# A two-layer Mamba-and-experts kernel: layer 0's first sequence ahead of the rest, other rows and the router between scan units, idle TensorE products at the start, an expert per six units

## The chip, the cores and the metric

The kernel runs on one core of one Trainium2 chip, in fp32 apart from small counts in bf16. The metric is the device time of one execution in microseconds, the median over runs. A core has five engines that run side by side, each with an instruction queue of its own worked in order: TensorE (PE: matrix products, whose weight loads are listed as PEld), VectorE (DVE), ScalarE (ACT), GpSimd (POOL) and SyncE (SP), which here only issues transfers. They wait for each other through semaphores.

## The reference, cut to what matters

The input x is 8 sequences of 256 tokens with 128 features, 2048 rows in all. Two layers follow each other. In both, the normalized x goes through an attention-like part and a mixture of experts, and both are added to x. Layer 0 has a selective state-space model (256 channels, 16 states each) and 8 experts that each choose 512 tokens; layer 1 has a retention block and 16 experts, of which each token chooses two. The change is in layer 0:

```
xn = _layernorm(x)                     # outer norm
x = x + _L0_attn_ref(xn, ...) + _L0_ffn_ref(xn, ...)

# _L0_attn_ref, X = xn
Xn = (X - mu) * rsqrt(var + 1e-05) * ln_g + ln_b         # inner norm
X_main = einsum('bld,ed->ble', Xn, W_up1)
X_main = silu(causal_conv4(X_main, conv_w) + conv_b)
pp = einsum('bld,ed->ble', X_main, W_ll) + b_ll
delta = softplus(pp[..., :D]); Bm = pp[..., D:D+N]; Cm = pp[..., D+N:]
A = -exp(A_log)
A_bar = exp(delta * A)
U = X_main * (A_bar - 1) / (delta * A) * delta * Bm
for t in range(256):                   # the scan
    H = A_bar[t] * H + U[t]
    y[t] = sum_n(C[t] * H)
Y = y * silu(einsum('bld,ed->ble', Xn, W_up2))
out = X + einsum('bld,ed->ble', Y, W_down) + b_down

# _L0_ffn_ref, xt = rows of xn
scores = softmax(xt @ Wr)              # 2048 x 8, the router
G, idx = top_k(scores.T, 512)          # each expert takes 512 rows
h = gelu(xt[idx] @ W1 + b1); X_e = h @ W2 + b2
out = zeros.at[idx].add(G * X_e)
```

## The kernel before

`block_kernel` writes both layers into one program. Layer 0 is written under a manual schedule: on PE, ACT, DVE and POOL the instructions stand in the order in which the Python code emits them. Only SP's transfers are ordered by the tile framework. Line numbers below are those of the kernel before.

**Ahead of the scan.** SP loads x in four parts (L187) and then the parameters, one after the other. DVE takes mean and variance of the 16 row blocks of 128 rows (L233, L234). ACT and DVE make `rs` and, for the second norm inside the state-space part, `nm` and `rv`. For each quarter of the rows (512 rows, two sequences) ACT writes the inner norm `xh` and DVE the outer norm `xn`; PE transposes both; `XnT` (for the state-space part) and `xnT` (for the router) are the copies out of PSUM. `xn` goes to DRAM (`xn_d`), from which experts later gather rows. POOL prepares `wcv`, the four convolution taps times the up projection, and `dg`, diagonal matrices with 1/A. Then come the router's products (`pl`, L736), its softmax, and the search.

**The search** (`search`, L427) finds each expert's 512th score in ten steps of three bits: DVE makes seven candidates, compares all scores (`ge`) and adds them up (`cp`), PE adds over partitions (`pc`), and DVE keeps what still has 512 rows (`keep`, `m`, `thr`). Then it ranks the chosen rows. It is a Python generator: each `next` emits the part up to the next `yield`. In the same way `front(q)` (L303) emits the front of block q (two sequences) in ten parts: convolution products `pu`, gate products `pg`, silu, `pd` for delta, `pbc` for B and C, the softplus, `BT` with B transposed, and `xT` and `xS`, the transposed inputs. ACT needs one function table for silu, another for exp and ln, and another for gelu; each change of table is an instruction of its own.

**Units.** The loop `for k in range(len(units) + 4)` at the end of layer 0 runs over 64 units: 8 sequences, 4 groups of 4 states, 2 halves of the channels. A unit is a pipeline over several passes of the loop: `spread_b` (POOL, `Bd`), `decays` two passes ahead (ACT, `ab`), `x_times_b` one pass ahead (PE, `u`), `steps` (DVE: `u` times `ab - 1`, then the scan into `h`), `times_c` one pass later (POOL), `sums` two passes later (PE, `py`). After eight units `gated` and `down` finish a sequence. C comes back from DRAM spread over all partitions (`Cb`, three buffers).

Beside the unit each pass emits one part of each generator in `running`: the search, `base` (POOL adds xn and a bias to x, which is then written to `acc_d`), a front (block 1 from pass 0, 2 from 17, 3 from 33), and `select(e)`, which every `PACE` = 5 passes starts to find and gather expert e's rows. As soon as the first expert's rows are there, each pass also emits a part of `experts()`: five parts per expert, the first with both halves of the hidden layer, then four output products; results are scattered with addition into `acc_d` by POOL. Six of the ten search steps are emitted ahead of the loop, between parts of `front(0)`.

**Shared storage.** `bank()` gives PSUM tiles out of two buffers, shared by fronts, router, search, select and experts; `u` has two PSUM buffers of its own, `ab` three and `h` four in SBUF. `x` and `xn` share their SBUF place with the hidden tiles `ht` of the experts, `xh` and `xnT` with the experts' gathered rows `XgT`.

Layer 1 follows (from L839): it reads `acc_d` back, when all scatters have landed.

Of the kernel before, what the change touches and what calls it, by code (L numbers as in the profile page):

```python
# [8 lines left out]
F32 = mybir.dt.float32  # L9
# [16 lines left out]
K = 4  # L26
# [16 lines left out]
SB = 3  # L43
BK = 64
# [6 lines left out]
def block_kernel(ctx: ExitStack, tc: tile.TileContext, a: dict, out: bass.AP):  # L51
# [98 lines left out]
    with ExitStack() as l0:  # L150
# [13 lines left out]

        def exp_and_ln():

            nc.scalar.add_instruction(
                mybir.InstLoadActFuncSet(
                    name=nc.get_next_instruction_name(), act_func_set_id=EXP_LN, ins=[], outs=[]
                )  # L170
            )
# [16 lines left out]
        alog = load0("alog", [P, ND, N], a["alog"].rearrange("(c p) n -> p c n", p=P))  # L188
# [6 lines left out]
        ln_g = load0("ln_g", [P, 1])  # L195
        ln_b = load0("ln_b", [P, 1])
        wr0 = load0("wr0", [P, E0])
        conv_b = load0("conv_b", [P, ND])
# [6 lines left out]
        wup2 = load0("wup2", [P, D])  # L205
        wll = load0("wll", [P, ND, D + 2 * N], a["wll"].rearrange("(c p) e -> p c e", p=P))
        bll_d = load0("bll_d", [P, ND])
        bll_bc = load0("bll_bc", [2 * N, 1])
# [16 lines left out]
        exp_and_ln()  # L225
        nc.scalar.activation(An, alog, AF.Exp)
        nc.scalar.activation(sd[:, 0:1], eps_t, AF.Sqrt)
        nc.gpsimd.memset(XnT[:, :, 0 : K - 1], 0.0)
        for c in range(NC):
            if c == 8:  # L230
                nc.vector.tensor_scalar(An, An, -1.0, None, ALU.mult)
                nc.vector.reciprocal(rA, An)
            nc.vector.bn_stats(st[:, c, :], x[:, c, :])  # L233
            nc.vector.bn_aggr(mv[:, c, :], st[:, c, :])  # L234
        nc.scalar.activation(sd, mv[:, :, 1], AF.Sqrt, bias=eps_t)

        for dc in range(ND):
            for n in range(0, N, 8):
                nc.gpsimd.tensor_tensor(
                    dg[:, dc, n : n + 8], bc(eye, 1, 8), bc(rA[:, dc, n : n + 8], 2, BK), ALU.mult  # L240
                )
        nc.gpsimd.tensor_tensor(wcv, bc(wup1, 1, K), conv_w, ALU.mult)
        rs = main.tile([P, NC], F32, name="rs")
        nc.vector.reciprocal(rs, sd)
        vi = main.tile([P, NC], F32, name="vi")
        nc.vector.tensor_mul(vi, mv[:, :, 1], rs)
        nc.vector.tensor_mul(vi, vi, rs)
        nc.scalar.activation(vi, vi, AF.Sqrt, bias=eps_t)
        nm = main.tile([P, NC], F32, name="nm")
# [24 lines left out]
        for h in range(2):  # L274
            for g in range(2):
                q = 2 * h + g
                cols = slice(q * BLK, (q + 1) * BLK)
                for c in range(4 * q, 4 * q + 4):
# [4 lines left out]
                    if c:  # L283
                        normalize(c)
# [1141 lines left out]
```

## Time and profile before

The median of three runs is 700.51 us (699.24 to 701.1).

| what | us |
|---|---|
| profiled execution, its own time | 702.32 |
| its span, first to last instruction | 700.4 |
| first scan unit starts | 68.0 |
| unit 8 (search done) starts | 123.5 |
| unit 17 starts | 165.0 |
| last scan (unit 63) starts | 431.4 |
| layer 1 reads x back (`x<-acc_d`) | 442.6 |

Busy time in us in four stretches:

| stretch | length | PE | DVE | ACT | POOL |
|---|---|---|---|---|---|
| 0 to 41.5 | 41.5 | 22.3 | 23.1 | 16.3 | 8.8 |
| 41.5 to 68.0 | 26.5 | 21.0 | 19.1 | 16.4 | 8.0 |
| 68.0 to 123.5 | 55.5 | 42.2 | 51.7 | 26.4 | 32.4 |
| 345.9 to 395.8 | 49.9 | 46.5 | 35.9 | 30.1 | 44.7 |

A line of the list of groups names the source line, engine, operation and tiles (out <- in), how many there are, then busy time and the mean in ns, then the idle time just ahead of them and who ended most of it. A line of the timeline begins with start and duration in us; in brackets stands how long the engine was idle and who released it. In the page's rows of digits each digit is the busy share of one fortieth of the span in tenths.

### The profile page before, as it was taken

Reading aid. Unit: us, or ns where it says so; the run is one execution under the profiler, and the core shown is the slowest. Engines: PE = TensorE matmul, PEld = TensorE weight load, DVE = VectorE, ACT = ScalarE, POOL = GpSimd, SP = SyncE. Lnnn points to the kernel's source line nnn. Section 1 sums busy time; section 2 is a strip of 40 time slices with the busy share of each in tenths; the row PEclk is TensorE's granted clock in tenths of the full one; section 3 lists DMA queues with packets and bytes.
Section 4 is the critical chain, followed back from the end, with each engine's and each line's share of the span. In section 5 each row is a group of like instructions: output and inputs, shape, how many; then the busy total and the mean of one; then the engine's idle time right before and its main releaser. Section 6 shows DMA issues by size and latency. Waiting matters only on the chain.

```text
span 700.4 us, 14519 instructions
## 1 busy us (share of the span) xinstructions
PE 560.8 (80%) x5721; PEld 427.5 (61%) x5721; DVE 428.2 (61%) x669; ACT 332.5 (47%) x763; POOL 381.8 (55%) x320
## 2 busy tenths in 40 slices
PE   0997777789889798989798867497639899999980
PEld 0765545667666776756675756364215498999870
DVE  7367998997647578465666887565117532454333
ACT  2546355556677574677374731243003243555530
POOL 5004646698868789873999896106740022444340
PEclk9997887789989899998898987567558888999995
DMA  7813002222692343321332220122424246888306
GB/s 206 106 24 122 32 31 103 82 78 71 143 181 67 95 108 80 85 60 50 84 96 76 60 80 2 60 91 87 153 84 152 71 128 210 286 276 288 139 27 183
DMA packets 59859, 76.27 MB, mean 109 GB/s; under 512 B 14992, under 2 KB 43808, under 8 KB 59536
## 3 DMA queue, kind: packets, MB, share of 16 engines
q1 hardware_dynamic: 51632, 65.81, 32.6%
q0 software_dynamic: 8160, 9.54, 6.4%
q8 instruction: 45, 0.74, 0.4%
q14 instruction: 22, 0.18, 0.1%
HBM read 59.46 MB, written 13.78 MB: 105 GB/s over the span
## 4 chain that ended last, share of the span: by engine, by line
PE 34%; DVE 10%; issue 9%; POOL 7%; ACT 3%; DMA 2%; SPq 0%; POOLq 0%; DVEq 0%; ACTq 0%
PE ph L1175 6%; PE py L1189 5%; PE py L705 3%; POOL h L696 3%; PE ps L1008 3%; PE u L670 2%; PE pret L1028 2%; DVE u L688 2%; PE ph L603 2%; PE po L621 2%; DVE h L692 2%; POOL acc_d L569 2%; DMA y<-y_d 1%; POOL xg L546 1%; DVE st L1015 1%
## 5 line engine op out<-in xcount | busy, mean ns | idle before, releaser
L696 POOL TENSOR_TENSOR h<-h,Cb 128x1024 f32<-128x1024 f32 x64 | 172.2, 2727 | 32.3 <-DVE h L692 17.4
L692 DVE TENSOR_TENSOR_SCAN h<-ab,u 128x1024 f32<-128x1024 f32 x64 | 146.4, 2287 | 6.3 <-DVE ab L690 0.5
L680 ACT ACTIVATE ab<-delta,An 128x256 f32<-128x256 f32 x256 | 108.5, 498 | 23.2 <-DVE h L692 22.3
L1195 POOL DMA_INDIRECT y_d<-yo,xt x47 | 45.4, 967 | 119.1 <-DVE yo L1194 107.9
L688 DVE SCALAR_TENSOR_TENSOR u<-ab,u 128x1024 f32<-128x1024 f32 x64 | 78.0, 1218 | 48.1 <-PE u L670 33.1
L705 PE MATMUL py<-h,dg 64*64 64x128 f32 x2048 | 81.6, 302 | 23.0 <-POOL h L696 17.3
L670 PE MATMUL u<-Bd,xT 64*128 64x128 f32 x512 | 84.7, 311 | 12.2 <-DVE h L692 11.5
L670 PEld LDWEIGHTS u<-Bd,xT 64*128 64x128 f32 x512 | 71.1, 212 | 29.0 <-issue 14.1
L705 PEld LDWEIGHTS py<-h,dg 64*64 64x64 f32 x2048 | 64.0, 148 | 33.2 <-POOL h L696 21.1
L670 PE MATMUL u<-Bd,xS 64*128 64x128 f32 x512 | 82.3, 312 | 1.2 <-DMA xS<-xT 1.2
L1180 ACT ACTIVATE hid<-ph,wb 128x128 f32<-128x128 f32 x188 | 53.6, 368 | 51.9 <-issue 21.4
L670 PEld LDWEIGHTS u<-Bd,xS 64*128 64x128 f32 x512 | 68.7, 211 | 1.7 <-DMA xS<-xT 1.5
L569 POOL DMA_INDIRECT acc_d<-oc,idx x32 | 51.6, 1611 | 25.5 <-ACT oc L626 19.7
L1015 DVE TENSOR_TENSOR st<-ps,decay_sb 128x384 f32<-128x384 f32 x64 | 31.2, 548 | 52.6 <-remote 29.4
L1175 PE MATMUL ph<-xT,wb 128*128 128x128 f32 x376 | 53.6, 288 | 3.3 <-DVE xT L1169 2.7
L1124 POOL DMA_INDIRECT xs_d<-xk,pos x32 | 32.1, 1002 | 41.9 <-DVE hit L1106 32.5
L1175 PEld LDWEIGHTS ph<-xT,wb 128*128 128x128 f32 x376 | 48.8, 202 | 5.9 <-DVE xT L1169 3.1
L1189 PE MATMUL py<-wb,hid 128*128 128x128 f32 x376 | 51.2, 281 | 0.0
L654 POOL TENSOR_TENSOR Bd<-eye,BT 128x256 f32<-128x256 f32 x64 | 50.5, 992 | 0.0
L1189 PEld LDWEIGHTS py<-wb,hid 128*128 128x128 f32 x376 | 47.3, 198 | 0.0
L621 PEld LDWEIGHTS po<-w,ht 128*128 128x128 f32 x256 | 35.9, 209 | 14.9 <-issue 5.2
L621 PE MATMUL po<-w,ht 128*128 128x128 f32 x256 | 40.5, 303 | 4.5 <-ACT BT L388 2.8
(257 smaller groups left out, 900.9 us busy)
## 6 DMA issues: line engine op xcount, KB each, us to landing
wb<-in_bank_dram SPq DMA_DIRECT2D x47, 514.0 KB
Cb<-C_d SPq DMA_DIRECT2D x32, 512.0 KB
w<-in_w_dram SPq DMA_DIRECT2D x16, 256.0 KB
xs_d<-zrow SPq DMA_DIRECT2D x1, 3031.5 KB
xt<-xs_d SPq DMA_DIRECT2D x11, 260.0 KB
xS<-xT SPq DMA_DIRECT2D x16, 128.0 KB
y<-y_d SPq DMA_DIRECT2D x8, 256.0 KB
decay_sb<-in_decay_dram SPq DMA_DIRECT2D x1, 1536.0 KB
```

Source lines behind the costliest of these rows:

```text
L569: i = nc.gpsimd.indirect_dma_start(out=acc_d, out_offset=bass.IndirectOffsetOnAxis(ap=idx[:, e, s : s + 1], axis=0), in_=oc, in_offset=Non ...
L621: nc.tensor.matmul(po, ht[:, hc, s * P : (s + 1) * P], w2[:, hc, :], start=(hc == 0), stop=(hc == NH - 1),)
L654: nc.gpsimd.tensor_tensor(t[:, w], eye.unsqueeze(1).unsqueeze(1).to_broadcast([P, 2, 2, BK]), bc(BT[b // 2][:, j + 2 * i : j + 2 * i + 2, ...
L670: nc.tensor.matmul(U[k][:, 2 * r : 2 * r + 2, t0 : t0 + BK], xT[b][r ^ half][rows, c, dc * P : (dc + 1) * P], Bd[b, g][rows, 2 * c + half] ...
L680: nc.scalar.activation(ab[k][:, n, :], delta[b // 2][:, dc, (b % 2) * L : (b % 2 + 1) * L], AF.Exp, scale=An[:, dc, g * NG + n : g * NG + ...
L688: nc.vector.scalar_tensor_tensor(U[k], ab[k], -1.0, U[k], ALU.add, ALU.mult)
L692: return nc.vector.tensor_tensor_scan(hf, af, uf, 0.0, ALU.mult, ALU.add)
L696: nc.gpsimd.tensor_mul(hh[k][:, w], hh[k][:, w], Cb[b, g][:, w])
L705: nc.tensor.matmul(pyv[cols, i, dc, :], dg[rows, dc, g * NG + n, :], hh[k][rows, n, j * P : (j + 1) * P], start=(g == 0 and dc == 0 and n ...
L1175: nc.tensor.matmul(ph[:, hc, :], w[:, hc * P : (hc + 1) * P], xTs[t], start=True, stop=True)
L1180: nc.scalar.activation(hids[t][:, hc, :], ph[:, hc, :], AF.Relu, bias=w[:, DI + NH * DM + hc : DI + NH * DM + hc + 1],)
L1189: nc.tensor.matmul(py, hids[t][:, hc, :], w[:, DI + hc * DM : DI + (hc + 1) * DM], start=(hc == 0), stop=(hc == NH - 1),)
```

## The change

It does five things.

1. The start is cut. The first four row blocks get their variances and deviations ahead of the other twelve, only their `xh` and `XnT` are made, and `front(0, (0,))` emits the front of sequence 0 alone; its two `xS` copies are made by DVE out of PSUM instead of two transfers, and its gates come after the decays of units 0 and 1. Products on `ident` (`WARM` = 24) stand at the head of PE's queue. `wcv` and the parameter loads are ordered for this, `An`, `rA` and `dg` come after the first `pd`.
2. The front of sequence 1, `front(0, (1,))`, runs in the loop from pass 0; block 1's starts at pass 4 instead of 0.
3. A generator `others()` emits the other rows' norms and transposes, the router and all ten search steps inside the loop. The copies of `xnT` move from DVE to ACT.
4. While the search runs, each generator in `running` emits two parts per pass instead of one. `base` starts only after it.
5. `PACE` is 6; experts emit five parts in six passes, and the sixth has none.

By this, selecting begins at pass 10 (before: 8) and the first expert at pass 18 (before: 15).

```diff
--- before.py
+++ after.py
...
 ROW1 = DM + 2
...
-        alog = load0("alog", [P, ND, N], a["alog"].rearrange("(c p) n -> p c n", p=P))
+        ln_g = load0("ln_g", [P, 1])
+        ln_b = load0("ln_b", [P, 1])
         wup1 = load0("wup1", [P, D])
...
-        ln_g = load0("ln_g", [P, 1])
-        ln_b = load0("ln_b", [P, 1])
+        conv_b = load0("conv_b", [P, ND])
+        alog = load0("alog", [P, ND, N], a["alog"].rearrange("(c p) n -> p c n", p=P))
+        wll = load0("wll", [P, ND, D + 2 * N], a["wll"].rearrange("(c p) e -> p c e", p=P))
+        bll_d = load0("bll_d", [P, ND])
+        bll_bc = load0("bll_bc", [2 * N, 1])
+        wup2 = load0("wup2", [P, D])
         wr0 = load0("wr0", [P, E0])
-        conv_b = load0("conv_b", [P, ND])
...
-        wup2 = load0("wup2", [P, D])
-        wll = load0("wll", [P, ND, D + 2 * N], a["wll"].rearrange("(c p) e -> p c e", p=P))
-        bll_d = load0("bll_d", [P, ND])
-        bll_bc = load0("bll_bc", [2 * N, 1])
...
-        exp_and_ln()
-        nc.scalar.activation(An, alog, AF.Exp)
...
         nc.scalar.activation(sd[:, 0:1], eps_t, AF.Sqrt)
         nc.gpsimd.memset(XnT[:, :, 0 : K - 1], 0.0)
-        for c in range(NC):
-            if c == 8:
-                nc.vector.tensor_scalar(An, An, -1.0, None, ALU.mult)
-                nc.vector.reciprocal(rA, An)
+        nc.gpsimd.tensor_tensor(wcv, bc(wup1, 1, K), conv_w, ALU.mult)
...
+        def variance(c):
             nc.vector.bn_stats(st[:, c, :], x[:, c, :])
             nc.vector.bn_aggr(mv[:, c, :], st[:, c, :])
-        nc.scalar.activation(sd, mv[:, :, 1], AF.Sqrt, bias=eps_t)
-
-        for dc in range(ND):
...
-        nc.gpsimd.tensor_tensor(wcv, bc(wup1, 1, K), conv_w, ALU.mult)
...
-                transposes(h, 4 * g, xn, "xn")
-                nc.scalar.activation(
-                    XnT[:, 2 * q : 2 * q + 2, K - 1 :],
...
-                nc.vector.tensor_copy(
-                    xnT[:, cols], pts[h, "xn"][:, 4 * g : 4 * g + 4, :].rearrange("p j l -> p (j l)")
...
+        def deviations(cs):
+            nc.scalar.activation(sd[:, cs], mv[:, cs, 1], AF.Sqrt, bias=eps_t)
+            nc.vector.reciprocal(rs[:, cs], sd[:, cs])
+            nc.vector.tensor_mul(vi[:, cs], mv[:, cs, 1], rs[:, cs])
+            nc.vector.tensor_mul(vi[:, cs], vi[:, cs], rs[:, cs])
+            nc.scalar.activation(vi[:, cs], vi[:, cs], AF.Sqrt, bias=eps_t)
...
+        def inner(c):
+            nc.scalar.activation(
+                xh[:, c, :], x[:, c, :], AF.Identity, bias=nm[:, c : c + 1], scale=rv[:, c : c + 1]
+            )
...
+        def inner_rows(c0, n, name):
...
+            pt = bank(f"pt_xh{name}", [P, n, P])
+            for j in range(n):
+                nc.tensor.transpose(pt[:, j, :], xh[:, c0 + j, :], ident)
+            nc.scalar.activation(
+                XnT[:, c0 // 2 : (c0 + n) // 2, K - 1 :],
+                pt.rearrange("p (b j) l -> p b (j l)", j=2),
+                AF.Identity, bias=ln_b, scale=ln_g,
+            )
...
+        def outer(q):
+            for c in range(4 * q, 4 * q + 4):
+                nc.vector.tensor_scalar(
+                    xn[:, c, :], x[:, c, :], mv[:, c, 0:1], rs[:, c : c + 1], ALU.subtract, ALU.mult
+                )
...
+        def outer_rows(q):
+            pt = bank(f"pt_xn{q}", [P, 4, P])
+            for j in range(4):
+                nc.tensor.transpose(pt[:, j, :], xn[:, 4 * q + j, :], ident)
+            nc.scalar.copy(xnT[:, q * BLK : (q + 1) * BLK], pt.rearrange("p j l -> p (j l)"))
...
+        warm = bank("warm", [P, P])
+        for _ in range(WARM):
+            nc.tensor.matmul(warm, ident, ident, start=True, stop=True)
+        for c in range(4):
+            variance(c)
+        deviations(slice(0, 4))
+        for c in range(4, NC):
+            variance(c)
+        for c in range(2):
+            inner(c)
+        inner_rows(0, 2, "0a")
+        for c in range(2, 4):
+            inner(c)
+        deviations(slice(4, NC))
+        inner_rows(2, 2, "0b")
+
         xn_dv = xn_d.rearrange("(p c) d -> p c d", p=P)
-        nc.sync.dma_start(xn_dv[:, :, 0:DM], xn)
...
-        def front(q):
...
+        def front(q, hs=(0, 1)):
+
+            h0, n = hs[0], len(hs)
...
+            at_once = q == 0 and h0 == 0
+            if h0 == 0:
...
-                for h in range(2):
+                for h in hs:
...
-                        xq[:, dc, h * L : (h + 1) * L], pu, AF.Silu if q == 0 else AF.Identity,
...
-            if q:
-                for f in (
-                    xq.rearrange("p d l -> p (d l)"), gq.rearrange("p i d b l -> p (i d b l)")
...
+            if not at_once:
+                gates()
+                yield
+                nc.scalar.activation(xq[:, :, ts], xq[:, :, ts], AF.Silu)
+                silu_gates()
...
-            dq = main.tile([P, ND, BLK], F32, name=f"delta{q}", tag="delta", bufs=2)
...
+            z = main.tile([P, ND, BLK], F32, name=f"z{q}_{h0}", tag="z")[:, :, 0:W]
...
-                nc.sync.dma_start(xSb[0:BK], xTb[BK:P])
-                nc.sync.dma_start(xSb[BK:P], xTb[0:BK])
+                if at_once:
+                    nc.vector.tensor_copy(xSb[0:BK], px[BK:P])
+                    nc.vector.tensor_copy(xSb[BK:P], px[0:BK])
+                else:
+                    nc.sync.dma_start(xSb[0:BK], xTb[BK:P])
+                    nc.sync.dma_start(xSb[BK:P], xTb[0:BK])
                 xT[b] = xTb, xSb
-                if i == 0:
-                    nc.gpsimd.tensor_sub(dq, dq, z)
-                    yield
+                if i == h0:
+                    (nc.vector if at_once else nc.gpsimd).tensor_sub(dq, dq, z)
+                    if n == 2:
+                        yield
             nc.vector.tensor_add(dq, dq, w)
+            if at_once:
+                yield
+                gates()
+                silu_gates()
+                exp_and_ln()
             yield
...
-        pl = bank("pl", [P, NC, E0])
...
-        exp_and_ln()
-        nc.scalar.activation(ex, ex, AF.Exp)
-        sm = main.tile([P, NC], F32, name="sm")
...
-        find = search()
-        next(find)
-        for i, _ in enumerate(front(0)):
-            if i % 2 and i < 10:
-                next(find)
-        spread_c(0, 0)
-        spread_b(0, 0)
-        spread_b(0, 1)
-        decays(0)
-        x_times_b(0)
-        decays(1)
+        def others():
+            for q in range(1, 4):
+                for c in range(4 * q, 4 * q + 4):
+                    inner(c)
+                inner_rows(4 * q, 4, str(q))
+                outer(q - 1)
+                outer_rows(q - 1)
+                yield
+            outer(3)
+            outer_rows(3)
+            nc.sync.dma_start(xn_dv[:, :, 0:DM], xn)
+            yield
+            pl = bank("pl", [P, NC, E0])
...
+            nc.scalar.activation(ex, ex, AF.Exp)
+            yield
...
+            nc.vector.memset(thr, 0)
+            yield from search()
...
-        running = [find, base()]
...
+        for i, _ in enumerate(front(0, (0,))):
+            if i == 2:
+                nc.scalar.activation(An, alog, AF.Exp)
...
+                        nc.gpsimd.tensor_tensor(
...
+            if i == 5:
+                spread_c(0, 0)
+                spread_b(0, 0)
+                spread_b(0, 1)
+                decays(0)
+                x_times_b(0)
+                decays(1)
+        find = others()
+        running = [front(0, (1,)), find]
+        START = {4: front(1), 17: front(2), 33: front(3)}
         SEL0 = None
         chosen = 0
-        PACE = 5
+        first = None
+        PACE = 6
         work = experts()
         for k in range(len(units) + 4):
             if k in START:
...
-                running.insert(0, f(q))
+                running.insert(0, START[k])
...
-            part = next(work, None) if 0 in XgT else None
+            part = None
+            if first is None and 0 in XgT:
+                first = k + 1
+            if first is not None and k >= first and (k - first) % PACE < 5:
+                part = next(work, None)
...
-                if next(t, 0) == 0:
-                    running.remove(t)
-                    if t is find:
-                        SEL0 = k + 1
+                for _ in range(2 if SEL0 is None else 1):
+                    if next(t, 0) == 0:
+                        running.remove(t)
+                        if t is find:
+                            SEL0 = k + 1
+                            running.append(base())
+                        break
```

## The prediction

> **What bounds the kernel now.** First the row of slices and the costliest groups of the page, then busy times by stage, then single stretches in order of time.
>
> ```profile
> DVE  7367998997647578465666887565117532454333
> ...
> L696 POOL TENSOR_TENSOR h<-h,Cb 128x1024 f32<-128x1024 f32 x64 | 172.2, 2727 | 32.3 <-DVE h L692 17.4
> L692 DVE TENSOR_TENSOR_SCAN h<-ab,u 128x1024 f32<-128x1024 f32 x64 | 146.4, 2287 | 6.3 <-DVE ab L690 0.5
> ...
> L688 DVE SCALAR_TENSOR_TENSOR u<-ab,u 128x1024 f32<-128x1024 f32 x64 | 78.0, 1218 | 48.1 <-PE u L670 33.1
> ```
>
> A scan unit costs VectorE one u (1.22 us) and one scan (2.29 us); where nothing else waits, scans start 3.65 us apart (units 58 to 63). I read off the scan starts (L692): unit 0 at 68.0, 8 at 123.5, 10 at 135.3, 17 at 165.0, 63 at 431.4. Layer 1 follows, 269.0 us to the end.
>
> ```profile
> 68.00:123.50 55.50, 42.15 (x431) 30.36 (x430) 51.69 (x72) 26.36 (x51) 32.38 (x23) 0.81 0.17 62
> ...
> 345.90:395.80 49.90, 46.49 (x600) 34.31 (x592) 35.87 (x33) 30.05 (x67) 44.73 (x33) 0.90 0.30 75
> ```
>
> The columns are window, length, then PE, weight loads, DVE, ACT, POOL. In units 0 to 7, where the search runs, VectorE is busy 51.7 of 55.5 us: it is the bound there. Among the experts PE (46.5 of 49.9) and POOL (44.7) are full instead. So work handed to early units costs VectorE time one for one, unless VectorE had been idle; and ahead of unit 0 VectorE was not the bound.
>
> ```profile
> 13.89 2.31 DVE L246 TENSOR_TENSOR vi<-mv,rs 128x16 f32<-128x16 f32 x1
> ...
> 28.83 6.83 PE L736 MATMUL pl<-wr_sb,xnT 128*128 128x8 f32 x32
> 29.02 1.28 ACT L167 ACT_TABLE_LOAD   x1
> ...
> 35.52 6.63 PE L314 MATMUL pu<-XnT,wcv 128*128 128x256 f32 x16
> ...
> 39.32 0.47 ACT L318 ACTIVATE xm<-pu,conv_b_sb 128x256 f32<-128x256 f32 x1 [1.35 <-PE pu L314]
> ...
> 42.71 3.73 PE L314 MATMUL pu<-XnT,wcv 128*128 128x256 f32 x16 [0.54 <-ACT xm L318]
> 43.22 1.09 DVE L433 TENSOR_TENSOR ge<-sc,py 128x896 bf16<-128x896 f32 x1
> 44.34 1.09 DVE L439 TENSOR_REDUCE cp<-ge 128x56 bf16<-128x896 bf16 x1
> ```
>
> These are the prices of what moves: router products 6.8 us, two convolution groups 6.6 us on a slow PE and 3.7 on a fast one, a table load 1.28, and a search step, from keep to the end of cp, 3.2 us.
>
> **Part 1: the way to the first scan gets shorter.** The first four row blocks' variances end at 5.2 (first at 3.65, 0.39 each). Five small constants still stand there (2.6 us): 7.8. The deviation chain took 4.1 us (13.27 to 17.34), 2.1 of them because vi (2.31 instead of 0.18) ran beside wcv on POOL; wcv again falls there: 11.9. The other twelve variances (4.7) and their square roots (1.9) stand ahead of the second XnT copy on ACT: 19.0. The convolution groups of sequence 0 need only the first copy, so PE runs them from about 13.5 meanwhile; silu waits for ACT: a table load, two xm, a table load: 22.5. Four readings of pd (0.47 each), An, exp, 1+z, BC: 26.3. z, ln, BT, xT, xS and delta, each with one hand-over: 31.3. Decays 1.7, u 1.22: the first scan at **34.5** (32 to 40), 33.5 us earlier.
>
> **The idle products.** 24 products are 48 passes of 128 columns, by the 256-column pass of L314 (0.41 us slow) about 0.2 us each, so 10 us from about 1.6: they end near 12, as the first transposes are ready. The granted clock in the page reads 9 from the start, but L314's 6.63 against 3.73 shows a slow PE until about 39 us, so the row decides what cold costs: 1.5 us per group. The Trainium skill ("TensorE: Matmul & The Clock Gate", Part 1) says that some 3.4 us of work brings full clock and an idle window of the same length takes it away again. By the rule the groups run fast, 13.5 to 17.2; by the slow row they end at 20.1. ACT is ready for them at 20.3 in both cases, so its list covers the gain; behind it PE has idled again when pd comes. I take 0 (range 0 to 4, if pd, pbc and the transposes stay fast).
>
> **Part 2: VectorE's list in units 0 to 9.** Units 10 x 3.65 = 36.5. xn: 16 x 0.28 = 4.4. Router 1.9. Ten search steps x 3.2 = 32.0 (six stood ahead of the loop). Two rankings, slot and casts 3.1 + 4.2 + 0.3 + 3.9. First gate 0.7. Halves of sequence 1 and of block 1: 3.6. Sum **90.6**, so scan 10 could start at 125.1 if VectorE never waited; before it was 135.3. The transfers pass with it: both xn_d writes now go behind the Cb reads on SP, yet their first reader (xg, unit 11) is far off.
>
> **Part 3: where VectorE waits.** ACT's list between the decays of units 1 and 4 now holds, in its order: gates with two table loads 4.4, decays 1.7, xm 0.9, two quarters of xh, XnT, xnT 6.2, decays 1.7, gates and silu with two loads 5.1, relu and abs 0.9, the last quarters 3.8, decays 1.7: 26.4 us from 34.8, 61.2 without a wait, 63.3 with PE's hand-overs. Router products need the last xnT copy and stand on PE behind u of unit 3, sums, pd and pbc: they start at 66.0 and take 3.6 (fast) to 6.8 (slow); I take 4.5, to 70.5. VectorE, whose queue has the router's maximum ahead of u of unit 3, was done at 53.3: **17.2 idle**, 0.4 for ex, and 4.8 before u of unit 2 (behind xh's transposes on PE). Then two search steps per unit: the second needs the count of the first back from PE, 0.9 x 5 = 4.5. Between two units PE must do u, sums and two front pieces, and two PSUM banks pass between front, transposes and counts: waits of 0.9, 1.3, 0.9, 3.3, 0.4 and 3.5 in units 3 to 8 (the 3.3 is gate copy, table load, silu, pd in one unit), 10.3. Sum 37.2: scan 10 at **162.3**.
>
> Net table loads: seven against five before the experts, four of them among units. The row says 1.28 each and the next activation starts at once; the Trainium skill ("ScalarE: Activation LUTs", What ACT_TABLE_LOAD costs) adds a drain, 2.66 in all. By the rule ACT's list grows by 5.5; I take the row.
>
> **Part 4: the rest.** Units 10 to 63 took 296.1 (135.3 to 431.4). The eight base additions (1.27 each, 10.2 in all) move from units 0 to 7, where POOL had 23 idle us, to 10 to 17, where it has gathers too: 2.36 + 0.6 + 1.27 + 0.6 = 4.8 us per unit against 4.24 measured, +4.5. acc_d is written at unit 18 (issued at 118.1 before, its packets ran some 4 us). The first scatter, at 20, waits for it on POOL, and expert 0's ht, which takes x's place in SBUF, on ACT at unit 18, with the decays of unit 20 and the silu of block 2 behind it: 0 to 5, I take 2. Experts at six units instead of five: over the 3.65 floor an expert cost 5.3 to 8.1, the same work in both; a rest unit can absorb on POOL 3.65 - 2.36 - 0.6 = 0.7, so 0 to 8 for eight, I take 4. The tail behind scan 63 keeps its length: the last scatter (1.6 us) now goes out behind the last times_c, some 4 us after that scan, and 8.8 us lay between the scan's end and the reading of acc_d (442.6). Sum 296.1 + 4.5 + 2 - 4 = 298.6: scan 63 at 460.9, +29.5. With 269.0 behind it the span is 729.9. The profiled execution took 702.32 for a span of 700.4, 1.8 above the median of the runs, so the median follows the span: 700.5 + 29.5 = **730**.
>
> **Rivals.** *B, only the floor:* fast PE, ACT ahead of schedule, half of the 37.2 goes: +11, 711. For it: PE will be better fed and so faster; against: ACT's 26.4 us are sums of rows, no wait in them. *C, faster:* the collisions of fronts 2 and 3 with experts (units 17 to 26 took 71.0, 33 to 42 took 70.4, which is 42 over the floor and two experts each at 6.5) dissolve at six units per expert. It decides when over 29.5 of the 42 go; all gone gives 688. For it: units of 12.5 and 11.7 us there look like pile-ups. Against: PE is busy 10 us in each of them, and work stays. *D, worse:* two PSUM banks with more tenants hold PE at every unit of 3 to 9 for another 2 us: 745. *E, the warm-up holds:* the clock lasts through the front: 4 less, 726; inside my range.
>
> **How the numbers follow.** Mine 0.58, with E inside (716 to 742), B 0.20, C 0.11, D 0.11. No change within 0.3% (2.1 us, about the spread of the runs shown) is the seam between B and C: 0.03. Faster 0.10, slower 0.87. Eight in ten: from under B at 705 to past D at 749.
>
> **What would show it.** First scan near 34; VectorE idle about 17 us ahead of the router's maximum at 70; units 3 to 7 about 11 to 13 us apart; scan 10 near 162 and 63 near 461; the first convolution groups done before ACT takes them. I am wrong if units 0 to 9 take under 95 us (waits were hidden), or if units 17 to 42 get shorter by tens.

## The result and the profile after

The changed kernel takes 741.29 us (median of four runs, 739.43 to 746.76), the kernel before 699.88 in the runs beside it: a ratio of 1.060 (1.054 to 1.066), 41 us slower. The profiled execution has a span of 740.1. Against the prediction's steps, with starts of scans read from L719:

| stretch | before | predicted | after |
|---|---|---|---|
| start to first scan | 68.0 | 34.5 | 32.5 |
| units 0 to 9 | 67.3 | 127.8 | 129.9 |
| units 10 to 63 | 296.1 | 298.6 | 307.1 |
| from scan 63 to the end | 269.0 | 269.0 | 270.6 |
| span | 700.4 | 729.9 | 740.1 |

The head gives back 35.5 us; units 0 to 9 cost 62.6, units 10 to 63 another 11.0, the end 1.6. That is +39.7, the difference of the spans.

The row of slices and the costliest groups of the page after, as they were shown of before:

```profile
DVE  4563885789744476745969676466303554355342
...
L723 POOL TENSOR_TENSOR h<-h,Cb 128x1024 f32<-128x1024 f32 x64 | 174.9, 2743 | 73.0 <-DVE h L719 47.9
L719 DVE TENSOR_TENSOR_SCAN h<-ab,u 128x1024 f32<-128x1024 f32 x64 | 146.3, 2286 | 5.6
...
L715 DVE SCALAR_TENSOR_TENSOR u<-ab,u 128x1024 f32<-128x1024 f32 x64 | 78.0, 1219 | 60.5 <-PE u L697 50.2
```

VectorE's scans and u take the same time to a tenth of a microsecond, and POOL's product with C only 2.7 us more. What has grown is the idle time in front of them: ahead of POOL's product from 32.3 to 73.0 us, ahead of VectorE's u from 48.1 to 60.5. The busy time by stretch (window, length, then PE, weight loads, DVE, ACT, POOL) for units 0 to 2, 3 to 7 and 8 and 9 of the kernel after:

```profile
32.50:73.40 40.90, 31.34 (x232) 23.64 (x229) 21.92 (x36) 28.65 (x59) 8.15 (x5) 0.71 0.27 81
73.40:139.90 66.50, 41.24 (x329) 29.48 (x327) 50.00 (x80) 22.51 (x42) 16.84 (x12) 0.68 0.09 29
139.90:162.40 22.50, 12.89 (x144) 10.93 (x140) 17.70 (x24) 6.21 (x14) 9.44 (x6) 0.65 0.18 46
```

VectorE is busy 89.6 us of these 129.9 and idle 40.3. The prediction had 90.6 of list and 37.2 of waits. In units 3 to 7 no other engine is full either (PE 41 of 66.5), so the idle time is waiting for one another, not a second bound. Single rows of the timeline after (start, length, in brackets the idle time before it and its releaser):

```profile
40.33 5.25 DVE L275 TENSOR_SCALAR xn<-x,mv,rs 128x128 f32<-128x128 f32 x8
...
63.53 3.74 PE L775 MATMUL pl<-wr_sb,xnT 128*128 128x8 f32 x32
...
67.31 0.29 DVE L779 TENSOR_REDUCE mx<-pl 128x16 f32<-128x128 f32 x1 [16.37 <-PE pl L775]
...
83.94 0.22 DVE L474 TENSOR_SCALAR keep<-pc 128x56 int32<-128x56 f32 x1 [0.32 <-PE pc L469]
...
114.30 1.28 ACT L360 ACT_TABLE_LOAD   x1
115.59 1.06 ACT L360 ACTIVATE xm<-xm 128x1024 f32<-128x1024 f32 x1
...
120.56 0.22 DVE L474 TENSOR_SCALAR keep<-pc 128x56 int32<-128x56 f32 x1 [7.04 <-PE pc L469]
```

The router's maximum holds VectorE 16.4 us; a second search step waits only 0.3 for its own count; one count, behind a delta product that waits for a silu on ScalarE, costs 7.0.

The same in sums: VectorE's waits (tile and line, then releaser, us in total, times, longest). First before:

```profile
DVE u L688 <- PE u L670: 33.1, 10, 8.7
...
DVE ol L520 <- PE py L705: 13.2, 5, 6.2
...
DVE mx L740 <- PE pl L736: 5.9, 1, 5.9
...
DVE keep L447 <- PE pc L442: 5.1, 5, 1.7
```

and after:

```profile
DVE u L715 <- PE u L697: 50.2, 16, 8.8
...
DVE ol L547 <- PE py L732: 21.5, 6, 5.1
...
DVE mx L779 <- PE pl L775: 16.4, 1, 16.4
DVE keep L474 <- PE pc L469: 12.7, 9, 7.0
```

Each of the four has grown: u by 17, the selection's first comparison `ol` by 8 (by 4, if 4.5 us that it waited for u before are counted too), the router's maximum by 10, the search's counts by 8. The experiments take them one at a time.

### The profile page after: what moved, and what is told of

Its sections match the earlier page's. It is cut to its first block, busy times and chain, and to the rows that moved or that the text cites. A ratio compares the mean times of both kernels' runs of the same rounds, so it can differ in the third digit from the quotient of the medians.

```text
span 740.1 us, 14723 instructions
## 1 busy us (share of the span) xinstructions
PE 577.5 (78%) x5797; PEld 440.4 (60%) x5797; DVE 430.9 (58%) x677; ACT 341.3 (46%) x792; POOL 380.8 (51%) x320
## 3 DMA queue, kind: packets, MB, share of 16 engines
q1 hardware_dynamic: 51488, 65.55, 30.6%
## 5 line engine op out<-in xcount | busy, mean ns | idle before, releaser
L723 POOL TENSOR_TENSOR h<-h,Cb 128x1024 f32<-128x1024 f32 x64 | 174.9, 2743 | 73.0 <-DVE h L719 47.9
L719 DVE TENSOR_TENSOR_SCAN h<-ab,u 128x1024 f32<-128x1024 f32 x64 | 146.3, 2286 | 5.6
L715 DVE SCALAR_TENSOR_TENSOR u<-ab,u 128x1024 f32<-128x1024 f32 x64 | 78.0, 1219 | 60.5 <-PE u L697 50.2
L732 PE MATMUL py<-h,dg 64*64 64x128 f32 x2048 | 84.5, 310 | 29.4 <-POOL h L723 22.3
L697 PE MATMUL u<-Bd,xT 64*128 64x128 f32 x512 | 88.1, 319 | 5.8 <-DVE h L719 3.8
L732 PEld LDWEIGHTS py<-h,dg 64*64 64x64 f32 x2048 | 66.8, 154 | 39.5 <-POOL h L723 24.3
L697 PE MATMUL u<-Bd,xS 64*128 64x128 f32 x512 | 86.0, 319 | 1.9 <-issue 1.6
L697 PEld LDWEIGHTS u<-Bd,xT 64*128 64x128 f32 x512 | 74.1, 219 | 21.8 <-issue 9.8
L697 PEld LDWEIGHTS u<-Bd,xS 64*128 64x128 f32 x512 | 72.3, 219 | 2.5 <-issue 1.9
L1071 DVE TENSOR_TENSOR st<-ps,decay_sb 128x384 f32<-128x384 f32 x64 | 31.2, 548 | 56.0 <-remote 32.2
L1180 POOL DMA_INDIRECT xs_d<-xk,pos x32 | 32.0, 1001 | 41.6 <-DVE hit L1162 32.2
```

What stands on the lines that cost most here:

```text
L697: nc.tensor.matmul(U[k][:, 2 * r : 2 * r + 2, t0 : t0 + BK], xT[b][r ^ half][rows, c, dc * P : (dc + 1) * P], Bd[b, g][rows, 2 * c + half] ...
L715: nc.vector.scalar_tensor_tensor(U[k], ab[k], -1.0, U[k], ALU.add, ALU.mult)
L719: return nc.vector.tensor_tensor_scan(hf, af, uf, 0.0, ALU.mult, ALU.add)
L723: nc.gpsimd.tensor_mul(hh[k][:, w], hh[k][:, w], Cb[b, g][:, w])
L732: nc.tensor.matmul(pyv[cols, i, dc, :], dg[rows, dc, g * NG + n, :], hh[k][rows, n, j * P : (j + 1) * P], start=(g == 0 and dc == 0 and n ...
```

## The experiments

Kernels sent together ran on one chip. Chips differ: in the group of the router's maximum, the second half and the two combined kernels the kernel before took 663.9 us, in the other groups 696 to 700; there the part behind scan 63 took 231 to 241 us instead of 265 to 271. So times are compared as ratios to before, and inside layer 0 by scan starts. The lengths in the table are those of the profiled executions, as differences of rounded scan starts. The pace is six in the changed kernel, the one without idle products and the one with own tables, and five in all others.

| kernel | ratio to before | first scan | units 0-2 | 3-9 | 10-16 | 17-62 | scan 63 |
|---|---|---|---|---|---|---|---|
| before | 1 | 68.0 | 20.4 | 46.9 | 29.7 | 266.4 | 431.4 |
| changed | 1.060 | 32.5 | 40.9 | 89.0 | 33.6 | 273.5 | 469.5 |
| no idle products | 1.066 | 33.8 | 41.1 | 89.2 | 33.5 | 276.9 | 474.5 |
| pace five | 1.046 | 30.7 | 40.4 | 91.5 | 29.2 | 266.2 | 458.0 |
| one search step per unit | 1.028 | 30.6 | 37.8 | 67.7 | 46.9 | 264.8 | 447.8 |
| router's maximum later | 1.040 | 33.2 | 28.2 | 95.6 | 32.6 | 263.0 | 452.6 |
| second half later | 1.031 | 34.3 | 29.7 | 92.7 | 29.2 | 265.4 | 451.3 |
| combined | 1.017 | 31.0 | 29.2 | 66.7 | 47.0 | 262.2 | 436.1 |
| combined, later maximum | 1.048 | 32.8 | 21.6 | 74.1 | 46.0 | 282.1 | 456.6 |
| own tables | 1.076 | 33.5 | 41.0 | 90.9 | 43.8 | 271.8 | 481.0 |
| combined, own tables | 1.050 | 30.9 | 32.2 | 69.1 | 54.5 | 273.6 | 460.3 |
| combined, spread | 1.001 | 34.1 | 33.8 | 55.5 | 47.1 | 261.7 | 432.2 |

**No idle products.**

```diff
-        warm = bank("warm", [P, P])
-        for _ in range(WARM):
-            nc.tensor.matmul(warm, ident, ident, start=True, stop=True)
```

> The changed kernel without the 24 idle products, all else the same. My part 1 took their gain as 0, with ScalarE's list as the cover: then the time stays at 741, within 1 us, and the first scan at 32.5. The rival that the warm-up holds (step E) says that 4 us come back: 745, first scan near 36. From the trace of the changed kernel I lean between: there ScalarE waited 0.5 and 2.1 us for the convolution groups, so PE was the last of the two, and cold groups (6.63 instead of 5.41 us) cost +1 to +3: first scan 33.5 to 35.5.

Measured 743.09 us (1.060 to 1.072), the first scan at 33.8, 1.3 later. The two kernels' intervals overlap. The first sequence's convolution takes 6.66 us instead of 5.41 and is enough to warm PE itself: the delta products behind it take 2.29 us in both. The gain is about 1 us here, and section "What the runs showed of the hardware" says when it is 3.

**Pace five.**

```diff
-        PACE = 6
+        PACE = 5
```

> The changed kernel with an expert and a selection every five units again, all else the same. My part 4 credited the pace of six with -4: then this kernel takes 745. The rival, from the trace of the changed kernel (units 10 to 63 took 307.1 where I had 298.6, and the selection's first comparison waits 4.6 to 5.1 us for the sums in five units of ten): the pace of six spreads the collisions instead of absorbing them, and five gives 731 or less, units 10 to 63 near 297.

729.5 us (1.040 to 1.052) where the changed kernel had 741.3 (1.054 to 1.066): 12 us less, units 10 to 63 in 295.4 us instead of 307.1. The rival holds, and the prediction's -4 for the pace of six has the wrong sign. VectorE's waits with pace five:

```profile
DVE u L715 <- PE u L697: 45.2, 11, 11.4
...
DVE ol L547 <- PE py L732: 9.5, 5, 2.7
...
DVE ol L547 <- remote: 3.8, 1, 3.8
```

`ol` waits 13.3 us instead of 21.5 and u 45.2 instead of 50.2. What happens to `ol` under pace six shows in unit 52 of the changed kernel, first POOL's queue, then PE and VectorE:

```profile
408.93 0.99 POOL L573 DMA_INDIRECT xg<-xn_d,idx  x1 [0.16 <-DVE h L719]
410.23 0.95 POOL L573 DMA_INDIRECT xg<-xn_d,idx  x1 [0.30 <-DVE ab L717]
411.49 1.64 POOL L596 DMA_INDIRECT acc_d<-oc,idx  x1 [0.31 <-issue]
412.57 2.93 POOL L723 TENSOR_TENSOR h<-h,Cb 128x1024 f32<-128x1024 f32 x1
...
415.56 1.99 PE L732 MATMUL py<-h,dg 64*64 64x128 f32 x32 [4.58 <-POOL h L723]
...
417.61 0.69 DVE L547 TENSOR_TENSOR ol<-iota_f,py 128x512 bf16<-128x512 f32 x1 [5.08 <-PE py L732]
```

Two gathers and a scatter stand on POOL ahead of the product with C, PE's sums wait 4.6 us for that product, and `ol`, whose tables share the PSUM tile of the sums, stands behind the sums; u and the next scan are queued behind `ol`. With five passes per expert the same instructions meet in another phase. That the phase is what makes six dearer is read from the trace. One run below, the combined kernel with the later maximum, moves the selection against the experts; it speaks for this, but at pace five, so it is not shown for six.

**One search step per unit** (with pace five; block 0's down projection moves to unit 17, since it reads what the search leaves).

```diff
-        find = others()
+        find, late = others(), search()
...
-            yield from search()
+            running.append(late)
...
-                for _ in range(2 if SEL0 is None else 1):
+                for _ in range(2 if SEL0 is None and t is not late else 1):
...
-                        if t is find:
+                        if t is late:
```

> As the kernel with pace five, but the search goes one step per unit instead of two (its end moves from unit 9 to unit 17, the experts eight units later, and block 0's down projection from unit 12 to unit 17, which reads what the search leaves). My part 3 puts 4.5 us on the second step's round trip and 10.3 on waits between PE, PSUM banks and VectorE in units 3 to 8: then this kernel is 10 to 15 us faster than the one with pace five, and units 3 to 16 together take that much less. The rival: the early units are long because VectorE's list is long, whichever unit it lies in: the same time within 3 us, with units 10 to 16 near 6.9 us each instead of 3.65. A second rival: eight units fewer for the experts crowd the end: slower by 3 to 8.

717.34 us (1.023 to 1.033), 12 less than with pace five: the size of the first expectation, though units 3 to 16 together are only 6.1 us shorter and not 10 to 15. Units 3 to 9 take 67.7 instead of 91.5 and units 10 to 16 46.9 instead of 29.2: of 23.8 us saved early, 17.7 return later, as the first rival said of the steps themselves (6.7 us per unit, 3.65 and a step). The rest, with 2.6 in units 0 to 2 and 1.4 behind unit 16, is waiting that is gone: up to the last scan VectorE is busy 303.6 us here and 302.7 with pace five. The second rival, a crowded end, is not seen. What still waits, from this kernel's timeline:

```profile
64.85 0.29 DVE L779 TENSOR_REDUCE mx<-pl 128x16 f32<-128x128 f32 x1 [15.83 <-PE pl L775]
...
72.68 2.83 DVE L430 TENSOR_TENSOR delta<-delta,w 128x512 f32<-128x512 f32 x1 [1.45 <-POOL delta L427]
...
103.28 0.22 DVE L474 TENSOR_SCALAR keep<-pc 128x56 int32<-128x56 f32 x1 [5.08 <-PE pc L469]
```

The next four kernels are aimed at these three rows.

**The router's maximum a unit later** (pace five, two steps per unit).

```diff
                     pl[:, c, :], xnT[:, c * P : (c + 1) * P], wr0, start=True, stop=True
                 )
+            yield
+            yield
             mx = main.tile([P, NC], F32, name="mx")
```

> As the kernel with pace five, but the router's maximum, and all behind it, one unit later: VectorE does u and the scan of unit 3 while the router products run. My part 3 (VectorE stands idle because the maximum lies ahead of u of unit 3, whose operands are ready near 60): one floor of 3.65 goes into the idle, 3 to 4 us faster than pace five (722 to 727), and the idle ahead of the maximum falls from 16 to about 12. If u of unit 3 waits as long for PE or ScalarE as the maximum did, nothing: the same time within 1 us.

Ratio 1.040 (1.028 to 1.053) against 1.046 (1.040 to 1.052): the intervals overlap. In the traces units 0 to 9 take 123.8 us instead of 131.9, but units 10 to 16 take 32.6 instead of 29.2, since the search ends a unit later: 4.7 us less in all. The maximum no longer waits; most of its idle time changed places: u of unit 3 now waits 8.5 us for PE, the router's sum 3.4 for ScalarE, and the half front 2.9.

**The second half of sequence 0 later** (pace five, two steps per unit).

```diff
-        running = [front(0, (1,)), find]
+        half = front(0, (1,))
+        running = [find, half]
...
-                for _ in range(2 if SEL0 is None else 1):
+                n = 2 if SEL0 is None else 1
+                if t is half:
+                    n = {0: 0, 1: 0, 2: 3}.get(k, 5)
+                for _ in range(n):
```

> As the kernel with pace five, but the second half of sequence 0's front starts at unit 2, behind the router products, instead of unit 0. My part 3 says that ScalarE's list (26.4 us between the decays of units 1 and 4) sets the router: without the half's 7.3 us of ScalarE work, and its table loads, the products start 7 to 9 us earlier, the idle ahead of the maximum falls to 7 to 9, and what comes back in units 3 and 4 (the half must be done by unit 4) is 3 to 6: 1 to 6 us faster than pace five in all. The rival: a slow PE's chain (transposes, xnT copies) sets the router: the idle falls by under 3, and the time grows by 2 to 5, for the half's work lands in fuller units.

Ratio 1.031 (1.022 to 1.040), 1.5% or 11 us under pace five, more than expected. The idle time ahead of the router's maximum falls from 15.8 to 5.7 us, and units 0 to 9 take 122.4 instead of 131.9. So the half front, whose first reader is unit 8, did hold the router, as part 3 says.

**Combined.** Pace five, one step per unit, the half front behind the router, the search ahead of the fronts in each pass, and

```diff
-                    (nc.vector if at_once else nc.gpsimd).tensor_sub(dq, dq, z)
+                    (nc.vector if q < 2 else nc.gpsimd).tensor_sub(dq, dq, z)
```

> Pace five and one search step per unit, with the half of sequence 0 behind the router products, the search's count ahead of the fronts in PE's order (there the step waited 5.1 us in unit 6 and 2.9 in unit 4), and the subtraction for the decay steps on VectorE in sequences 0 and 1 (VectorE waited 1.5 and 2.5 us for POOL there and its own addition took 2.8 and 3.4 instead of 1.1 and 1.2 us). If each of these waits costs what the trace of the one-step kernel shows: 717 - 7 (router) - 8 (counts) - 6 (subtraction) = 696 to 700, level with the kernel before. If a removed wait only uncovers the next one: 706 to 717.

Ratio 1.017 (1.007 to 1.028), 1.0% under the one-step kernel where 2.4 to 2.9% were expected. The two intervals overlap; in the traces the last scan starts 11.6 us earlier (436.1 for 447.8). What VectorE waits for in it:

```profile
DVE z L391 <- ACT w L378: 11.2, 3, 5.0
...
DVE mx L779 <- PE pl L775: 7.5, 1, 7.5
...
DVE keep L474 <- PE pc L469: 4.7, 1, 4.7
DVE py L456 <- PE py L732: 4.0, 1, 4.0
```

The maximum waits 7.5 instead of 15.8, but unit 3, in which the half front is now squeezed, lasts 17.0: 4.0 of waiting for the sums (behind 6.6 us of convolution on PE) and 4.6 for the front's w.

**Combined, with the later maximum.** The two `yield` lines of above, in the combined kernel, and a second edit:

```diff
             if first is None and 0 in XgT:
-                first = k + 1
+                first = k
```

Expert 0's rows come a pass later here; with `first = k` the experts still begin at the same pass as in the combined kernel.

> As the combined kernel, and the router's maximum a unit later. By the floor that goes into the idle: 3 to 4 less than the combined kernel, 692 to 697. If the idle ahead of the maximum has gone already: the same within 1 us, or 1 to 3 more, as the search ends a unit later.

Ratio 1.048 (1.038 to 1.058): both expectations missed. The idle ahead of the maximum falls to 2.0, but the router's sum behind it waits 9.1 for `ex`, which stands on ScalarE behind the convolution's copies, and w another 6.4; unit 3 lasts 25.2, and scan 4 starts at 79.7 instead of 77.2, of which 1.8 are the head's. The larger loss, units 17 to 62 in 282.1 instead of 262.2, comes behind the search. There selection and base additions have moved a unit (`ol` runs in units 18, 23 and so on instead of 17, 22) and the experts have not; units 25 and 26 take 28.5 us instead of 18.1. In the run with only the router's maximum later, selection and experts moved together, and units 17 to 62 took 263.0 for pace five's 266.2. So moving the selection against the experts is the likelier cause. It isn't shown alone, for it moved against the fronts too.

**Own tables.** In the changed kernel and in the kernel before, thresholds and tables get a tile in SBUF instead of the unused halves of the sums' PSUM tile.

```diff
-        tab = py[:, 0, L:]
+        tabs = const.tile([P, 2, L], F32, name="tabs")
+        tab = tabs[:, 0, :]
...
-        tab1 = py[:, 1, L:]
+        tab1 = tabs[:, 1, :]
```

> The changed kernel (pace six, two search steps per unit) with one edit: the tables of search and selection have a tile of their own in SBUF instead of the free halves of the sums' PSUM tile. In the changed kernel the selection's first comparison waited 21.5 us for the sums in six units. If that shared tile is why units 10 to 63 grew by 11 instead of 2.5: most of those waits go, and the ratio to the kernel before falls from 1.060 to 1.030 to 1.045. If the comparison only waits where u or the scan would wait anyway (for a full POOL and PE): u waits as much more as the comparison waits less, ratio 1.055 to 1.062.

> The kernel before with the same edit, the tables in a tile of their own; there the selection's comparison waited 17.7 us in six units (13.2 for the sums, 4.5 for u). If the shared tile costs them: 5 to 15 us faster, ratio 0.979 to 0.993, faster than both kernels. If PE and POOL are the bound in those units: the same, 0.997 to 1.003; a little slower (1.003 to 1.01) if tables in SBUF make VectorE's steps slower beside POOL.

Both lose: 1.076 (1.067 to 1.085) where 1.060 was, and before itself 721.68 us, 1.035 (1.027 to 1.043). So the waits for the sums can't be priced with this edit, for it brings a larger cost. The groups of VectorE of the kernel before with own tables, from 60 us on (line, tiles, count, busy us, mean ns, idle before):

```profile
L521 DVE TENSOR_TENSOR ol<-iota_f,tabs 128x512 bf16<-128x512 f32 x8 | 15.1, 1882 | 0.0
L530 DVE TENSOR_TENSOR rr<-oh,tabs 128x256 bf16<-128x256 f32 x16 | 12.6, 824 | 0.3
L452 DVE SCALAR_TENSOR_TENSOR tabs<-m,tabs 128x8 int32<-128x8 int32 x6 | 10.8, 1808 | 0.2
```

With the tables in PSUM `ol` was 683 ns, `rr` 418, and the threshold step on eight numbers, of which six of ten fall here, 170. `ol`'s 17.7 us of waiting are gone, yet selection is busy 23 us longer, and units 10 to 63 end up at 298.5 against 296.1; units 0 to 9, with the search, take 83.0 instead of 67.3.

**Combined and spread, with own tables and without.** To the combined kernel: the half front's convolution at units 0 and 1, its gates and silu at unit 2, the rest at 3, and in both first fronts a pass between silu and the delta products.

```diff
                 silu_gates()
             exp_and_ln()
+            if q < 2 and not at_once:
+                yield
...
-                    n = {0: 0, 1: 0, 2: 3}.get(k, 5)
+                    n = {0: 1, 1: 1, 2: 2}.get(k, 5)
```

> The combined kernel of the run before (ratio 1.017), with the convolution of sequence 0's second half at units 0 and 1 and its silu at unit 2, silu and delta products a unit apart in the first two fronts (PE stood 3.1 us in unit 6 behind a delta product that waited for silu, and the count behind it 4.7), and the tables in a tile of their own. If each wait of unit 3 (4.0 + 4.6) and unit 7 (4.7) is worth what it shows: 8 to 13 us less than the combined kernel, ratio 0.998 to 1.006, units 3 and 7 at 8 to 11 and 7 us. If they only uncover the next wait: 1.012 to 1.02.

1.050 (1.043 to 1.057): the tables' cost again. Units 3 and 7 are 10.8 and 9.4 us.

> As the combined kernel with own tables, but with the tables back in the sums' PSUM tile. There the search's small threshold step took 2.1 instead of 0.17 us beside POOL, its comparison 1.4 to 3.2 instead of 1.1, the selection's ol 1.9 instead of 0.7: that is 18 to 20 us in the two kernels before with and without own tables, and 25 to 35 here, where the whole search lies among units. Against the first combined kernel (1.017) units 3 and 7 should fall from 17.0 and 11.5 to about 10.8 and 7 us: -8 to -11. Ratio 0.999 to 1.007. If the waits for the sums come back at the search's steps (4.0 us in one unit of the first combined kernel): 1.008 to 1.017.

699.86 us against 699.32, ratio 1.001 (0.997 to 1.005). Units 3 to 7 last 10.8 and four times 6.76, units 3 to 9 together 55.5 instead of 66.7, and no count waits. So the loss of the changed kernel is its waits and its pace: with them mended, 41 us come back. It is level with before, not better: its scan 17 starts at 170.5 against 165.0, and units 17 to 62 give 4.7 back. VectorE is idle 9.5 us ahead of the router's maximum still.

**Idle products in the kernel before**, 60 of them at the start of PE's queue.

```diff
+        warm = bank("warm", [P, P])
+        for _ in range(60):
+            nc.tensor.matmul(warm, ident, ident, start=True, stop=True)
```

> The kernel before with 60 idle products at the start of PE's list, nothing else. If they bring the clock and the stream of transposes keeps it: the router products take 3.7 instead of 6.83 us and the four convolution groups 1.9 less each; VectorE's search steps between cover part: 692 to 696 (6 less). If the clock is lost in the gaps before the router: 699 to 701, no change.

698.98 us, ratio 0.999 (0.996 to 1.003): nothing. PE's rows of this kernel:

```profile
1.62 16.18 PE L270 MATMUL warm<-ident 128*128 128x128 f32 x120 [1.62 <-POOL ident masks.py:199]
...
20.58 1.48 PE L276 MATMUL pt_xh<-ident,xh 128*128 128x128 f32 x4 [0.81 <-ACT xh L283]
21.90 0.60 PE L276 MATMUL pt_xn<-ident,xn 128*128 128x128 f32 x4
23.32 1.63 PE L276 MATMUL pt_xh<-ident,xh 128*128 128x128 f32 x4 [0.81 <-ACT xh L283]
24.74 1.06 PE L276 MATMUL pt_xn<-ident,xn 128*128 128x128 f32 x4
...
28.47 6.83 PE L740 MATMUL pl<-wr_sb,xnT 128*128 128x8 f32 x32
```

Four transposes take 0.60 us until 22 and 1.06 from 24 on. Between groups PE waits for `xh`, and the granted clock falls from 1.00 to 0.50 at 24.0 and stays there until 41: it is gone before the router, and `pl` takes its 6.83 us as ever. No version here beats the kernel before by more than the measurement tells.

## Why the prediction was right or wrong

**The outcome** lies in the range and on the likelier side: 741.3 for 730. The 10.2 us between the spans are -2.0 in the head, +2.1 in units 0 to 9, +8.5 in units 10 to 63 and +1.6 behind.

**Part 1** held as a sum: 32.5 for 34.5. Two of its terms were too long: the first deviations were done at 7.2 and not 11.9, as `wcv` came later and didn't run beside them, and ScalarE was ready for the convolution at 15.0 and not 20.3. Part of that was lost again in waits. The idle products' "gain 0" was near in size and wrong in reason. ScalarE's list didn't cover the convolution; it waited 0.5 and 2.1 us for it. The convolution ended at 18.0, between the 17.2 of a fast PE and the 20.1 of a slow one: the clock fell inside it, as the last section shows. What covers them is POOL: `wcv` waits for its parameter until 10.2 and ends at 12.6, so PE can't begin earlier, warm or not.

**Part 2** held as a sum, with errors that cancel: VectorE was busy 89.6 us for a list of 90.6, but `xn` took 7.4 for 4.4 and the two halves 8.0 for 3.6, while rankings, slot and casts took 7.6 for 11.5 and the search 30.3 for 32.0. This is the core of the result: the head shrinks by 35.5, and VectorE's early list, which before lay in part beside a head in which it had been idle, now lies bare.

**Part 3** held as a sum (40.3 idle for 37.2), less so in its terms. The router's maximum waited 16.4 for 17.2. The wait before u of unit 2 was 1.7 for 4.8, but the eight xn beside it took 5.25 us where I had 2.2. The round trip of a second step was 0.3 for 0.9; the front's chain of gate copy, table load, silu and delta product cost 7.0 for 3.3. The run with one step per unit took 12 us less, near the 4.5 + 10.3 of this part, but only 6.1 of that in units 3 to 16. For the table load the row was right: it began at 114.30 and its activation at 115.59, 1.29 later; the 2.66 that the Trainium skill gives ("ScalarE: Activation LUTs", What ACT_TABLE_LOAD costs) would have made it 116.96.

**Part 4 failed**, in the step "a rest unit can absorb on POOL 3.65 - 2.36 - 0.6 = 0.7, so 0 to 8 for eight, I take 4". The term is not -4 but about +12: 741.3 against 729.5, and 307.1 against 295.4 us in units 10 to 63. I counted what a free pass can absorb and not what the six-pass rhythm does to the waits: `ol` waited 8.2 us more and u 5.0 more than with pace five. Why it does so is read from unit 52 alone. The two terms taken as losses, 4.5 for the base additions and 2 for `acc_d` and x's place, aren't seen: with pace five units 10 to 63 take 295.4, under the 296.1 of before. These errors partly cancel, which is luck: the part is 8.5 us short where the pace alone was 16 off. For the changed kernel with pace five the same sum would have said 734 for 729.5.

**The rivals.** Of B, a better fed and faster PE, half is there: the router products took 3.74 us, the fast value, but the waits stayed. C, the collisions of units 17 to 42 dissolving at six units per expert, is refuted: these units took 172.0 us (196.0 to 368.0) against 171.1 (165.0 to 336.1). D's 2 us more in each of units 3 to 9 would have been 14; units 0 to 9 are 2.1 over the sum. E is neither: 1.3 us in this execution, and up to 3 in others.

## What to carry to other kernels

Work that is moved out of a head into a loop pays the head's gain only up to the list of the engine that bounds the loop: add that list up first, then look for the order in which each in-order queue waits, since mending the queues and the pace was worth 41 us here and reached level, no more. A front's long chain through another engine (copy, table load, silu, product) belongs a pass away from the short product that a bounding engine waits for. A rhythm of periodic jobs is to be tried on the chip in both directions: one pass more per expert cost 12 us although it only added free slots.

## What the runs showed of the hardware that was not expected

**Operands in PSUM kept VectorE clear of POOL.** Two rows of the timeline of the kernel before with own tables, POOL's product with C and, on VectorE, the search's threshold step on eight numbers:

```profile
79.48 2.36 POOL L697 TENSOR_TENSOR h<-h,Cb 128x1024 f32<-128x1024 f32 x1 [5.99 <-DVE h L693]
...
79.83 2.03 DVE L452 SCALAR_TENSOR_TENSOR tabs<-m,tabs 128x8 int32<-128x8 int32 x1
```

The step ends at 81.86, as POOL's product does (81.84). In the kernel before, with the table in PSUM, the same step beside the same product takes 0.17 us:

```profile
84.06 2.36 POOL L696 TENSOR_TENSOR h<-h,Cb 128x1024 f32<-128x1024 f32 x1 [1.96 <-DVE h L692]
...
84.46 0.17 DVE L451 SCALAR_TENSOR_TENSOR py<-m,py 128x8 int32<-128x8 int32 x1
```

The Trainium skill ("SBUF — State Buffer", Who interferes with whom) says that a VectorE instruction with two SBUF inputs contends with a GpSimd instruction that reads SBUF, for a pair of ports that only one of them can hold at a time; with own tables both are of this kind, and the numbers agree. A PSUM tile's spare half is thus not only storage: giving it up cost the kernel before 3.5%.

**How long the warm-up lasts hung on where the clock's steps fell.** In ten of these kernels PE's head is the same. The convolution of the first sequence (16 products) in PE's timeline of the one-step kernel:

```profile
12.38 3.78 PE L327 MATMUL pu<-XnT,wcv 128*128 128x256 f32 x16 [0.49 <-POOL wcv L238]
```

and in that of the spread kernel:

```profile
13.08 6.65 PE L327 MATMUL pu<-XnT,wcv 128*128 128x256 f32 x16 [2.08 <-POOL wcv L238]
```

In four traces (one-step, pace five, combined, combined with own tables) these products took 3.7 to 4.1 us, in three (changed, combined with later maximum, router's maximum later) 5.4, in three (own tables, spread, second half later) 6.3 to 6.7. The first scan follows: 30.6 to 31.0, then 32.5 to 33.2, then 33.5 to 34.3, where 33.8 is the kernel without idle products.

The granted clock shows when PE became slow. Here are two stretches of the changed kernel and two of the one-step kernel (columns as above, then the granted clock):

```profile
10.18:13.59 3.41, 1.63 (x7) 1.15 (x7) 2.50 (x15) 2.00 (x6) 2.38 (x1) 1.00 0.16 43
13.59:17.00 3.41, 3.41 (x10) 2.66 (x9) 0.24 (x2) 1.90 (x3) 0.00 (x0) 0.50 0.81 237
...
10.67:14.08 3.41, 2.36 (x10) 1.71 (x10) 2.51 (x16) 1.87 (x6) 1.65 (x1) 1.00 0.31 81
14.08:17.49 3.41, 3.33 (x16) 2.42 (x15) 0.12 (x2) 3.06 (x5) 0.00 (x0) 1.00 0.89 245
```

In each trace the changes of the clock in the first 42 us lie 3.41 us or a multiple of it apart (changed kernel: down at 13.59, up at 17.00, down at 23.83, up at 34.07). Where this series of steps begins differs from execution to execution. In the three traces with 5.4 us the clock fell at 12.8 to 13.6, inside the convolution, and for one step; in the three slowest at 11.4 to 12.2, before it, and for two; in the four fast ones not before 21. The step that ended in the fall had PE busy for 27 to 48%; in the four fast traces each step from 7 us on until the convolution was at 69% or more. A step of 70% ended in a fall in the kernel before with idle products, so the runs give no threshold. Idle time just ahead of the convolution sorts the ten runs in the same way (at most 0.72 us, 0.97 to 1.41, 1.83 to 2.43); the runs don't separate the two, but in the changed kernel the clock fell 1.0 us after that idle time was over. The idle products are worth 0 to 3 us by the execution.
